# Scores and exponential emitted one opening sooner in each slot of a sparse graph transformer

## The chip, the cores and the metric

The kernel runs on one core of a Trainium2 chip, as one launch. The metric is the device time of that launch in microseconds (us); lower is better. The time before is the median of 7 runs. Five engines work in parallel, each through its own queue in order: TensorE (PE in the profile, with its weight loads as PEld), VectorE (DVE), ScalarE (ACT), GpSimd (POOL) and SyncE (SP, which issues direct DMAs; the gathers are issued by POOL).

## The reference

Sixteen graphs share one sparse adjacency matrix of 1024 nodes (an edge with probability 1/128); every node has 128 features. Four layers follow each other: layers 0, 2 and 3 are attention over the neighbours with 8 heads of 16, layer 1 is a graph attention with one additive score. Cut to what matters, an attention layer is

```python
Q, K, V = (h @ Wq), (h @ Wk), (h @ Wv)          # 8 heads of 16
scores = einsum('bnhd,bmhd->bhnm', Q, K) / sqrt(16)
attn = softmax(where(adj == 0, -inf, scores))
x = layer_norm(h + einsum('bhnm,bmhd->bnhd', attn, V) @ Wo + bo)
x = layer_norm(x + relu(x @ W1 + b1) @ W2 + b2)
```

and layer 1 takes `leaky_relu(h @ a_src + (h @ a_dst).T)` as scores, with `h = x @ W`, and a layer norm after the residual.

## The kernel before, in words

`sparse_path` does the work (`dense_path` is there for matrices with too many neighbours, and is not entered here). It sorts the nodes by their degree into 8 tiles of 128 (`t`), so that the nodes of a tile have about as many neighbours, and handles the 16 graphs in two groups of 8 (`g`). Keys and values of all nodes lie in tables in DRAM; the neighbours' rows are gathered by index.

**Units and parts.** A unit is (layer, group, tile): 64 in all. Four neighbours of 32 nodes fill the 128 partitions (a "chunk"), and `ROUNDS` says how many chunks a tile needs. A part of an attention unit is two chunks (L531 to L534): the tiles of a group have 10, 6, 6, 6, 4, 4, 4 and 3 parts. There are 3 attention layers, so six such groups of 8 units, and 258 attention parts. Layer 1 has parts of four chunks.

**A slot** is one pass of the loop at L735. For an attention part `i` it emits:

1. `products(i)`, L600: VectorE multiplies the gathered keys by the replicated queries.
2. `weighted(i - 1, 0)`, L639: VectorE multiplies the gathered values of the part before by its exponentials.
3. `gathered(i + 2)`, L591: two gathers on POOL, for a buffer that an earlier part has left.
4. `others()`: an opening, here called the first one.
5. in the second slot of a unit: the rest of `closing`. This is `divided` of the unit before: after its denominators (L680, L685) a reciprocal (L687) and two multiplications (L690) on VectorE, an addition on POOL (L700), and the start of two tails, one for each half of the group. Then the load of `x` two units ahead (L546) and the start of `queries(u + 1)`.
6. `others()`: the second opening.
7. `exponentials(i)`: VectorE sums the products over each head (L614, the scores), ScalarE takes the exponential (L618).
8. `summed(i - 1)`, L666: PE adds the weighted values up over the chunks of a round. In the first slot of a unit the denominators of the unit before follow.
9. `others()`: the third opening.

**Tails and fronts.** What follows the attention of a unit (output projection, two layer norms, feed-forward, projection for the next layer's table) is a generator, `attention_tail`, cut by `yield` into some 16 steps; two run at a time, the second a step behind. `others` advances both, as often as `pace` has grown by 1 (L763 to L765: 16 steps spread over three openings per part of the unit), and one step of `queries` for the next unit. The steps, in order: transposition (L429) and its eviction (L431); output projection (L465, L466); bias (`y`, L469, VectorE); squares (L413, ScalarE, four activations); the power -1/2 (L419, POOL); scaling (L422, ScalarE) with the next transposition and eviction (L433); first feed-forward matrix (L479) and its evictions (L483); second matrix (L488, L492); squares, power and scaling again; eviction, and the table rows of the next layer (L371 and L375, or L391 to L400), or in layer 3 two multiplications on POOL and a scattered store (L446 to L448). `queries` makes four matmuls (L566), a copy (L570), four replications over the neighbours (L575) and four copies (L578), for each half.

**Order.** The loop stands under `tc.manual_schedule()`: every engine executes its instructions in the order in which the program emits them. An instruction that waits holds back all behind it on its engine.

Of the kernel before, what the change touches and what calls it, by code (L numbers as in the profile page):

```python
# [76 lines left out]
def sparse_path(ctx: ExitStack, tc: tile.TileContext, a: dict, out: bass.AP, flag):  # L77
# [434 lines left out]
    def first(g):  # L512

        for t in range(T):
            for h in range(HF):
                xg = ones_.tile([P, GH, D], F32, tag="xg", name="xg")
                nc.gpsimd.indirect_dma_start(
                    out=xg.rearrange("p g d -> p (g d)"), out_offset=None,
                    in_=a["x"].rearrange("n (k c) -> (n k) c", k=GR * HF),
                    in_offset=bass.IndirectOffsetOnAxis(ap=places[:, g, h, t : t + 1], axis=0),  # L520
                )
                xn = states.tile([P, GH, P], F32, tag="xT", name="xT")
                turned(xg, xn)
                yield
                yield from project(0, g, t, h, xn)
# [11 lines left out]
    def is_attention(u):  # L537
        return LAYERS[units[u][0]][1] is ATTN

    def loaded(u):  # L540

        if u >= len(units):
            return
        l, g, t = units[u]
        xs[units[u]] = inputs.tile([P, HF, GH, P], F32, tag="x", name="x")
        nc.sync.dma_start(  # L546
            xs[units[u]].rearrange("p h g n -> p (h g n)"),
            kept[l, g][t].rearrange("p h c -> p (h c)"),
        )

    def queries(u):

        l, g, t = units[u]
        if not is_attention(u):
            ps = bank([P, J, G])
            for j in range(J):
                nc.tensor.matmul(ps[:, j, :], rep_of(j, True), srcs[g, t], start=True, stop=True)
            ofs[u] = smalls.tile([P, J, G], F32, tag="of", name="of")
            nc.scalar.copy(ofs[u], ps)
            return  # L560
        qs[u] = reps.tile([P, J, ROW], F32, tag="qr", name="qr")
        for h in range(HF):
            q = ones_.tile([P, GH * D], F32, tag="q", name="q")
            ps = bank([P, GH, D])
            for i in range(GH):
                nc.tensor.matmul(  # L566
                    ps[:, i, :], xs[l, g, t][:, h, i, :], w[LAYERS[l][0], "Wq"],
                    start=True, stop=True,
                )
            nc.scalar.copy(q, ps.rearrange("p g d -> p (g d)"))  # L570
            yield
            pss = []
            for j in range(J):
                ps = bank([P, GH * D])
                nc.tensor.matmul(ps, rep_of(j), q[32 * j : 32 * j + 32], start=True, stop=True)  # L575
                pss.append(ps)
            for j in range(J):
                nc.scalar.copy(qs[u][:, j, h * GH * D : (h + 1) * GH * D], pss[j])  # L578
            yield

    def gathered(i):
        if i >= len(parts):
            return
        u, r, j, n = parts[i]
        l, g, t = units[u]
        width = tables[l, g].shape[1]
        many = 2 if is_attention(u) else J
        e = gather_buffer()
        es[i] = e[:, : many * width].rearrange("p (k c) -> p k c", k=many)
        for k in range(n):  # L590
            nc.gpsimd.indirect_dma_start(  # L591
                out=es[i][:, k, :], out_offset=None, in_=tables[l, g][:, :],
                in_offset=bass.IndirectOffsetOnAxis(ap=idx[:, t, j + k, r : r + 1], axis=0),
                bounds_check=N - 1, oob_is_err=False,
            )

    def products(i):
        u, r, j, n = parts[i]
        prs[i] = [prods.tile([P, 2, ROW], F32, tag="pr", name="pr")]
        nc.vector.tensor_tensor(  # L600
            prs[i][0][:, :n, :], es[i][:, :n, :ROW], qs[u][:, j : j + n, :], ALU.mult
        )

    def exponentials(i):
        u, r, j, n = parts[i]
        t = units[u][2]
        heads = H if is_attention(u) else 1
        sc = smalls.tile([P, es[i].shape[1], G * heads], F32, tag="sc", name="sc")
        if u not in exs:
            exs[u] = exps.tile([P, max(map(sum, ROUNDS)), G * heads], F32, tag="ex", name="ex")  # L610
        c = CHUNK[t, r, j] - CHUNK[t, 0, 0]
        ex = exs[u][:, c : c + n, :]
        if is_attention(u):
            nc.vector.tensor_reduce(  # L614
                sc[:, :n, :], prs[i][0][:, :n, :].rearrange("p k (a d) -> p k a d", d=HD),
                mybir.AxisListType.X, ALU.add,
            )
            nc.scalar.activation(ex, sc[:, :n, :], AF.Exp, scale=1.0 / HD**0.5)  # L618
        else:
            nc.vector.tensor_tensor(  # L620
                sc[:, :n, :], es[i][:, :n, ROW:], ofs[u][:, j : j + n, :], ALU.add
            )
            nc.vector.scalar_tensor_tensor(
                sc[:, :n, :], sc[:, :n, :], SLOPE, sc[:, :n, :], ALU.mult, ALU.max
            )
            nc.scalar.activation(ex, sc[:, :n, :], AF.Exp)
# [79 lines left out]
    def advance(gens):  # L706
        for gen in list(gens):
            if next(gen, "end") == "end":
                gens.remove(gen)
# [3 lines left out]
    def others():  # L713
        pace[0] += pace[1]
        while pace[0] >= 1.0:
            advance(tails)
            pace[0] -= 1.0
        if fronts:
            advance(fronts)
        elif slow:  # L720
            advance(slow)

    with tc.manual_schedule():
        for _ in first(0):
            pass
        loaded(0)
        loaded(1)
        for _ in queries(0):
            pass
        slow.append(first(1))  # L730
        for i in range(AHEAD):
            gathered(i)
        closing = None
        begun = 0
        for i in range(len(parts) + 1):  # L735
            here = i < len(parts)
            u = parts[i][0] if here else len(units)
            if here:
                l = units[u][0]
                if i and parts[i - 1][0] != u:  # L740
                    begun = i
                    if units[u][1:] == (0, 1) and l + 1 < len(LAYERS):
                        if LAYERS[l + 1][1] is ATTN:
                            load_weights(LAYERS[l + 1][0])
                if is_attention(u):
                    products(i)
                else:
                    exponentials(i)
            ends = i + 1 >= len(parts) or parts[i + 1][0] != u
            if i:  # L750
                weighted(i - 1, 0)
                if not is_attention(parts[i - 1][0]):
                    others()
                    weighted(i - 1, 2)
                gathered(i - 1 + AHEAD)
            others()
            if closing is not None:
                while tails:
                    advance(tails)
                for _ in closing:  # L760
                    pass
                closing = None
                passes = 3 if is_attention(u) else 4  # L763
                steps = STEPS if is_attention(parts[begun - 1][0]) else GRAPH_STEPS
                pace[:] = 0.0, steps / (passes * sum(part[0] == u for part in parts) - 1)  # L765
            if here and u + 1 < len(units):
                if i == begun + 1:
                    loaded(u + 2)
                    fronts.append(queries(u + 1))
            others()  # L770
            if here and is_attention(u):
                exponentials(i)
            if i:
                summed(i - 1)
                if parts[i - 1][0] != u:
                    closing = divided(parts[i - 1][0])
                    next(closing)
            others()
            if ends:

                while fronts:
                    advance(fronts)
        while tails:
            advance(tails)
        for _ in closing:
            pass
        while tails:
            advance(tails)
# [434 lines left out]
```

## Time and profile before

| what | value |
|---|---|
| time, median of 7 runs (lowest to highest) | 3025.26 us (3013.36 to 3031.94) |
| profiled execution: its own time | 3021.78 us |
| profiled execution: span from the first to the last instruction | 3020.0 us |
| mean granted clock of TensorE | 0.845 |
| preparation before the first attention part | about 259 us |
| score sums L614: number, busy | 258, 561.7 us |
| exponentials L618: number, busy | 258, 81.1 us |
| products with keys L600 and with values L639, busy | 565.0 us and 760.2 us |
| gathers L591: number, busy on POOL, from issue to landing | 656, 886.3 us, 7.6 us |

The page of a profile gives the busy time of each engine, then the span in 40 slices, the DMA queues, the chain of work that ended last (followed back from the last instruction, at each step to what released it), and groups of instructions by line. The list of waits gives for each pair of lines how long one engine sat idle until the other's work was there. The timeline gives the instructions in order of time; in brackets stands the idle time in front of an instruction and who ended it. A window gives, for one stretch, the busy time of PE, PEld, DVE, ACT and POOL, then TensorE's granted clock, the share of the DMA engines and GB/s. Line numbers are those of the kernel.

### The profile page before, as it was taken

The page shows a single profiled execution, that of the slowest core. Times are in us where ns is not written, and L with a number is a line of the kernel's source. Part 1 is how long each engine was busy: PE and PEld are TensorE (multiplying, and loading weights), DVE is VectorE, ACT ScalarE, POOL GpSimd, SP SyncE. Part 2 cuts the span into 40 slices and gives each one's busy share as a digit, 9 for nine tenths or more (in the row PEclk, how much of TensorE's full clock was granted, in tenths as well). Part 3 has the DMA queues.
Part 4 walks back from the last instruction along what each step waited for, and adds up shares of the span by engine and source line. Part 5 has one row for each costly group of instructions (what it writes and reads, how often), then busy time and mean ns, then how long its engine had stood idle before and what let it go on. Part 6 is the DMA issues. An engine that isn't in the chain of part 4 may idle for free.

```text
span 3020.0 us, 35305 instructions
## 1 busy us (share of the span) xinstructions
PE 2123.1 (70%) x12569; PEld 1320.3 (44%) x12569; DVE 2150.4 (71%) x1493; ACT 1424.2 (47%) x4468; POOL 1478.2 (49%) x1086
## 2 busy tenths in 40 slices
PE   1365667776777776776577887787877666766766
PEld 1343445443554443434245554455544444333444
DVE  7505758668886666675788768887678877788772
ACT  1033345563556544445345664456543554434454
POOL 0123434433444568786335443454435577466673
PEclk9986888888788888978688988889887888777887
DMA  1057866546565568777665654766546554355540
GB/s 57 12 179 288 298 226 231 182 170 229 222 239 184 174 208 292 272 268 274 226 235 215 230 207 174 278 221 226 204 183 246 200 201 154 152 221 212 195 144 22
DMA packets 171144, 615.36 MB, mean 204 GB/s; under 512 B 44472, under 2 KB 47928, under 8 KB 122462
## 3 DMA queue, kind: packets, MB, share of 16 engines
q0 software_dynamic: 99584, 480.93, 43.9%
q1 hardware_dynamic: 71376, 132.10, 11.9%
q8 instruction: 101, 1.65, 0.2%
q14 instruction: 83, 0.68, 0.1%
HBM read 650.67 MB, written 100.73 MB: 249 GB/s over the span
## 4 chain that ended last, share of the span: by engine, by line
PE 38%; ACT 14%; DVE 13%; POOL 10%; issue 10%; DMA 7%; POOLq 0%; DVEq 0%; SPq 0%; ACTq 0%
PE ps L479 7%; PE yps L488 5%; ACT z L413 5%; PE ps L429 5%; PE acc L666 5%; DVE pr L639 4%; POOL e L591 4%; DVE sc L614 4%; POOL rstd L419 4%; DMA e<-table,idx 3%; DVE pr L600 3%; ACT qr L578 3%; PE yps L465 3%; PE ps L575 3%; PE yps L492 3%
## 5 line engine op out<-in xcount | busy, mean ns | idle before, releaser
L591 POOL DMA_INDIRECT e<-table,idx x656 | 886.3, 1351 | 442.2 <-DVE pr L639 258.5
L639 DVE TENSOR_TENSOR pr<-e,ex 128x2048 f32<-128x2048 f32 (+1 forms) x344 | 760.2, 2217 | 334.9 <-ACT ex L618 329.4
L419 POOL TENSOR_TENSOR rstd<-total,power 128x4 f32<-128x4 f32 x224 | 359.1, 1605 | 744.5 <-ACT z L413 711.4
L600 DVE TENSOR_TENSOR pr<-e,qr 128x2048 f32<-128x2048 f32 (+1 forms) x258 | 565.0, 2190 | 190.6 <-ACT qr L578 138.4
L666 PE MATMUL acc<-pr,marks 128*32 128x512 f32 x2624 | 468.5, 701 | 142.5 <-DVE pr L639 131.8
L614 DVE TENSOR_REDUCE sc<-pr 128x128 f32<-128x2048 f32 (+1 forms) x258 | 561.7, 2177 | 0.0
L429 PE MATMUL ps<-ident,z 128*128 128x128 f32 x768 | 198.0, 365 | 241.9 <-ACT z L422 241.9
L429 PEld LDWEIGHTS ps<-ident,z 128*128 128x128 f32 x768 | 126.3, 171 | 393.0 <-ACT z L422 320.3
L479 PE MATMUL ps<-x,W 128*128 128x512 f32 x384 | 245.6, 773 | 39.9 <-ACT x L433 39.9
L371 PE MATMUL ps<-Wkv,xT 128*128 128x256 f32 x768 | 239.1, 457 | 39.1 <-ACT xT L431 21.1
L488 PE MATMUL yps<-W,f 128*128 128x128 f32 x1536 | 255.3, 284 | 12.6 <-ACT f L483 10.6
L666 PEld LDWEIGHTS acc<-pr,marks 128*32 128x32 f32 x2624 | 89.3, 120 | 394.0 <-issue 213.9
L488 PEld LDWEIGHTS yps<-W,f 128*128 128x128 f32 x1536 | 209.2, 194 | 68.4 <-ACT f L483 43.2
L483 ACT ACTIVATE f<-ps,b 128x512 f32<-128x512 f32 x192 | 131.4, 687 | 224.6 <-PE ps L479 223.9
L578 ACT COPY qr<-ps 128x512 f32<-128x512 f32 x384 | 197.5, 596 | 76.4 <-PE ps L575 76.3
L413 ACT ACTIVATE z<-y,root 128x128 f32<-128x128 f32 x512 | 198.5, 396 | 51.2 <-DVE y L506 37.9
L575 PE MATMUL ps<-q,rep 32*128 32x512 f32 x768 | 172.2, 687 | 66.7 <-ACT oT L431 40.4
L371 PEld LDWEIGHTS ps<-Wkv,xT 128*128 128x128 f32 x768 | 161.9, 225 | 86.9 <-ACT xT L431 29.5
L618 ACT ACTIVATE ex<-sc 128x128 f32<-128x128 f32 (+1 forms) x258 | 81.1, 314 | 248.6 <-DVE sc L614 248.4
L465 PE MATMUL yps<-Wo,oT 128*128 128x128 f32 x768 | 182.0, 325 | 7.5 <-ACT oT L431 7.5
L422 ACT ACTIVATE z<-y,rstd 128x128 f32<-128x128 f32 x512 | 162.7, 391 | 31.0 <-POOL rstd L419 31.0
L375 ACT COPY kv<-ps 128x512 f32<-128x512 f32 x192 | 112.3, 586 | 136.8 <-PE ps L371 132.9
(128 smaller groups left out, 2951.7 us busy)
## 6 DMA issues: line engine op xcount, KB each, us to landing
table<-kv SPq DMA_DIRECT2D x96, 512.0 KB, 8.6
kept<-xT SPq DMA_DIRECT2D x128, 256.0 KB, 5.6
x<-kept SPq DMA_DIRECT2D x64, 512.0 KB, 9.9
e<-table,idx POOLq DMA_INDIRECT x656, 7.6
table<-kv SPq DMA_DIRECT2D x32, 256.0 KB, 6.2
edges<-in_adj SPq DMA_DIRECT2D x8, 512.0 KB, 3.9
W<-in_L_gnn_W SPq DMA_DIRECT2D x6, 128.0 KB, 2.7
xg<-in_x,places POOLq DMA_INDIRECT x32, 4.1
```

The costliest lines, as they stand in the source:

```text
L371: nc.tensor.matmul(ps[:, k, :], x[:, i + k, :], w[LAYERS[l][0], "Wkv"], start=True, stop=True,)
L413: nc.scalar.activation(z[:, i, :], y[:, i, :], AF.Square, scale=D**-0.5, bias=root, accum_out=total[:, i : i + 1],)
L419: nc.gpsimd.tensor_tensor(rstd, total, power, ALU.pow)
L429: nc.tensor.transpose(ps[:, i, :], z[:, i, :], ident)
L479: nc.tensor.matmul(ps, p["W1"][:, f * P : (f + 1) * P], x1.rearrange("p g n -> p (g n)"), start=True, stop=True,)
L488: nc.tensor.matmul(ps[:, i, :], f1[:, f, i * P : (i + 1) * P], p["W2"][:, f, :], start=(f == 0), stop=False,)
L578: nc.scalar.copy(qs[u][:, j, h * GH * D : (h + 1) * GH * D], pss[j])
L591: nc.gpsimd.indirect_dma_start(out=es[i][:, k, :], out_offset=None, in_=tables[l, g][:, :], in_offset=bass.IndirectOffsetOnAxis(ap=idx[:, ...
L600: nc.vector.tensor_tensor(prs[i][0][:, :n, :], es[i][:, :n, :ROW], qs[u][:, j : j + n, :], ALU.mult)
L614: nc.vector.tensor_reduce(sc[:, :n, :], prs[i][0][:, :n, :].rearrange("p k (a d) -> p k a d", d=HD), mybir.AxisListType.X, ALU.add,)
L639: nc.vector.tensor_tensor(prs[i][k0 // 2][:, :m, :].rearrange("p k (a d) -> p k a d", d=d), es[i][:, k0 : k0 + m, base : base + ROW].rearr ...
L666: nc.tensor.matmul(accums[u][32 * j : 32 * j + 32, h, :], marks[:, CHUNK[t, r, j], :], tiles[j // 2][:, j % 2, h * GH * D : (h + 1) * GH * D],
```

## The change

The call of `exponentials(i)` for attention parts moves from behind the second opening to in front of it, ahead of the block that finishes the unit before and ahead of the start of the next queries. Nothing else changes; the parts of layer 1 emit their exponentials at the head of the slot, as before.

```diff
                 gathered(i - 1 + AHEAD)
             others()
+            if here and is_attention(u):
+                exponentials(i)
             if closing is not None:
                 while tails:
                     advance(tails)
...
                     loaded(u + 2)
                     fronts.append(queries(u + 1))
             others()
-            if here and is_attention(u):
-                exponentials(i)
             if i:
                 summed(i - 1)
                 if parts[i - 1][0] != u:
```

## The prediction

> **What bounds the kernel now.** I read the page first, then the list of waits, then the timeline of single units of nodes engine by engine, and the chain of waits inside such a unit. No engine is full:
>
> ```profile
> PE 2123.1 (70%) x12569; PEld 1320.3 (44%) x12569; DVE 2150.4 (71%) x1493; ACT 1424.2 (47%) x4468; POOL 1478.2 (49%) x1086
> ...
> PE 38%; ACT 14%; DVE 13%; POOL 10%; issue 10%; DMA 7%; POOLq 0%; DVEq 0%; SPq 0%; ACTq 0%
> ```
>
> The fullest engine works 71% of the span, and the chain that ended last (second line) passes through all of them: the time is a chain of hand-overs, and what a shift is worth depends on who waits at the place. The list of waits (engine and line, whom it waited for: total us, times, longest) has both sides of the moved step:
>
> ```profile
> DVE pr L639 <- ACT ex L618: 329.4, 126, 8.9
> ...
> ACT ex L618 <- DVE sc L614: 248.4, 72, 18.0
> ```
>
> VectorE waits 329 us for the exponential, because ScalarE still has tail work in front of it; ScalarE waits 248 us for the score sums, with its tail work behind. The change trades the first against the second.
>
> The timeline of a unit of six parts, ScalarE and then VectorE (start us, duration us, line, idle before and who ended it):
>
> ```profile
> 820.08 1.28 ACT L422 ACTIVATE z<-y,rstd 128x128 f32<-128x128 f32 x4 [0.21 <-POOL rstd L419]
> 821.37 0.31 ACT L618 ACTIVATE ex<-sc 128x128 f32<-128x128 f32 x1
> ...
> 827.34 0.78 ACT L433 ACTIVATE x<-ps,ln_b,ln_g 128x512 f32<-128x512 f32 x1
> ...
> 831.79 0.69 ACT L483 ACTIVATE f<-ps,b 128x512 f32<-128x512 f32 x1 [0.17 <-PE ps L479]
> 832.37 0.30 ACT L618 ACTIVATE ex<-sc 128x128 f32<-128x128 f32 x1
> ...
> 837.90 1.15 ACT L422 ACTIVATE z<-yps,rstd 128x128 f32<-128x128 f32 x4
> 838.90 0.35 ACT L618 ACTIVATE ex<-sc 128x128 f32<-128x128 f32 x1
> ```
>
> ```profile
> 819.06 2.28 DVE L614 TENSOR_REDUCE sc<-pr 128x128 f32<-128x2048 f32 x1
> ...
> 825.67 2.27 DVE L614 TENSOR_REDUCE sc<-pr 128x128 f32<-128x2048 f32 x1
> ...
> 832.70 2.29 DVE L639 TENSOR_TENSOR pr<-e,ex 128x2048 f32<-128x2048 f32 x1 [2.56 <-ACT ex L618]
> ...
> 839.31 2.28 DVE L639 TENSOR_TENSOR pr<-e,ex 128x2048 f32<-128x2048 f32 x1
> ```
>
> The exponential at 832.37 had its sums at 827.94 and stood behind two L483 evictions of the second opening, so VectorE lost 2.56. But the next one (838.90) follows tail squares, and no reordering around the second opening brings it before these.
>
> **The change part by part.** Nothing is added or removed: 258 score sums (L614, mean 2.28) and 258 exponentials (L618, 0.31) move ahead of the second opening, and in the second slot of a unit ahead of the closing block too. They issue no DMA and nothing on PE, POOL or SP; those queues keep their order. On VectorE they pass L687, two L690 and at times one L469; on ScalarE the second opening's evictions, squares and scalings. Behind the exponential now wait these, and for them PE and POOL. Busy sums: 0. The attention units are 6 groups of 8, with 10, 6, 6, 6, 4, 4, 4 and 3 parts (43 x 6 = 258), so I price each kind once.
>
> *Six parts (18 units).* At the start L687 and both L690 now stand behind a sum of 2.2. The transposed output's eviction L431 (804.06) stood behind that slot's exponential (803.85) anyway, and the new sequence brings it at 803.9: nothing, hidden by the exponential; without that cover 2.2. In the third slot the L422 scaling at 820.08 must now wait for the sum's end (821.34) and 0.31: 1.57 late. The product before it loses its own wait (0.45 behind the L578 copies), so 1.1. PE restarts 1.1 us earlier without the pause after its first L575 matmuls; its clock:
>
> ```profile
> 804.00:806.00 2.00, 1.32 (x2) 0.50 (x2) 2.00 (x2) 2.00 (x5) 0.00 (x0) 0.50 1.04 419
> ...
> 810.00:812.00 2.00, 2.00 (x20) 2.00 (x19) 1.65 (x2) 0.85 (x2) 0.99 (x1) 0.99 0.58 226
> ```
>
> (After the five engines' busy times comes the granted clock: 0.50 for six us from the restart, then 0.99.) Its four L465/L466 pairs take 0.85 each at 0.50 and 0.45 at 0.99, 1.6 in all; whether an unbroken restart saves them no row shows: between 0 and 1.6, I take 0.8. That leaves 0.3 of lateness. In the fifth slot the exponential comes straight after the squares (end 838.02), 0.9 sooner than 838.90. The 2.56 saved before is lost again there. Per unit -0.9 + 0.3 = -0.6, taken as -0.5; ends -1.5 (clock kept) and +0.7 (none of it: 1.57 - 0.9). In layer 3 the first product also waits for a gather behind POOL's output work: 0 there (-0.9 to +0.7). Sum 12 x -0.5 = -6 (-23 to +12).
>
> *Four parts (18 units).* The chain inside one such unit, then POOL's timeline:
>
> ```profile
> 569.38 1.55 ACT z L413 x8
> ...
> 588.55 0.99 POOL e L591
> 589.57 3.05 POOL rstd L419
> ```
>
> ```profile
> 569.06 1.03 POOL L419 TENSOR_TENSOR rstd<-total,power 128x4 f32<-128x4 f32 x1 [7.33 <-ACT z L413]
> ```
>
> The second tail's squares (569.28) now wait for the sum's end (570.02) and the exponential: 1.06 late, less 0.21 for the exponential that no longer follows them, 0.85. In layers 2 and 3 the same places give 1.77, and 1.5 after that exponential. Later in the unit an exponential moves from 584.66 to 578.9, and VectorE's 5.25 wait goes, but its next product still waits for scalings at 592.64. What is freed is the place where L600 ran: it moves from 589.42 to about 585, and the POOL power beside it at 589.57, on the chain with 3.05, could cost the 1.03 that one costs without a product beside it: -2.0. The first power now meets that product and pushes the gathers: +0.35. Net relief 1.65. Layer 0: 0.85 - 1.65 = -0.8; layer 2: -0.15; layer 3, with output work behind the powers, 0. Sum -6; ends per unit +1.5 (no relief) and -2.2 (the gather's 2.08 beside a product back to 0.99 too): -40 to +23.
>
> *Ten parts (4 of 6 units have tails to hide).* Here VectorE is the chain (its lines are over half of it from 2203 to 2240). Its 1.51 wait at 2217.51 goes, and the sum of the second slot finishes in the wait before: 1.45 more. ScalarE then holds an eviction (2232.37) behind a later sum; I take -2.4 of the -3.0. Sum -10 (-12 to 0).
>
> *Three parts (6).* L433 at 2177.12 waits for the sum's end 2178.06 and 0.31: 1.25 late, after 0.6 at the start; the last exponential comes 1.7 sooner. I take +0.6 (0 to 1.85): +4 (0 to +11).
>
> Total -6 - 6 - 10 + 4 = -18. The profiled execution took 3021.78 (span 3020.00 and 1.78 around it): 3003.8. The median of the runs is 3.5 above it: 3007.
>
> [...]
>
> **The rivals.** *VectorE gains its waits:* if the squares of the fifth slot came earlier, the six-part units would keep the waits (2.56 to 3.65, mean 3.0, 18 units: 54) and the ten-part units 10: 2961. For it: 329 us of waiting at L639. Against: the squares at 836.5 wait for PE.
>
> *A mere rotation:* in a steady unit each engine repeats the same sequence; if all gains and losses meet at the next wait, 3025. For it: the 2.56 above is lost six us later. That the move does not reach the chip is not likely: in the trace the exponentials stand exactly where the program emits them.
>
> *ScalarE blocked (slower):* the tail work behind the exponential sets the end and neither relief comes, POOL's second power staying near 3.0 and PE at 0.50 as now. Then 6 x 0.85 + 12 x 1.5 (four parts) + 6 x 1.85 (three) + 12 x 0.7 (six) = 43, less 10: +33, 3058. It decides as soon as the powers that follow the late squares still meet a product. For it: 711 us in which L419 waits for squares. Against: after the move VectorE has its products done by then.
>
> **How the numbers follow.** Forecast 0.39, VectorE's waits 0.09, rotation 0.16, ScalarE blocked 0.36. Predicted 3007, its own range 2985 to 3016. With the ends of the unknown costs (-75 to +46, so 2950 to 3071) and no more than 2 in 10 left out, the range is 2962 to 3062. A difference below 0.3% (9 us) can't be told from none here. Faster 0.39 + 0.09 = 0.48, same 0.16, slower 0.36.
>
> **What would show it.** Right: the waits of L639 for L618 fall below 150 us, those of L618 for L614 rise above 248; the second L419 in four-part units takes about 1 us; granted clock above 0.50 at the first L465 of six-part units; ten-part units some 2 us shorter. Wrong: four-part periods (40.7 now, the reciprocals at 558.0 and 598.7) grow; L429's wait for L422 (242 us) grows, which is the blocked tail; or six-part periods (48.4, L687 at 799.68 and 848.11) change by more than 1.5.

## The result and the profile after

The changed kernel takes 3037.03 us (median of 18 runs) against 3022.98 (46 runs of the kernel before): ratio 1.0048, 95% interval 1.0039 to 1.0058. It is slower by some 14 us. The profiled executions differ by 8.2 us (span 3020.0 and 3028.2).

The page after, busy time by engine and then the chain that ended last:

```profile
PE 2105.1 (70%) x12569; PEld 1314.8 (43%) x12569; DVE 2146.3 (71%) x1493; ACT 1425.3 (47%) x4468; POOL 1537.7 (51%) x1086
...
PE 37%; DVE 20%; issue 11%; ACT 10%; DMA 7%; POOL 6%; POOLq 0%; DVEq 0%; SPq 0%; ACTq 0%
```

VectorE and ScalarE have the work that they had; only the order has changed, and VectorE's share of the chain rose from 13% to 20%. POOL is busy for 59.5 us more, though its instructions are the same: the gathers L591 took 955.3 us in all (886.3 before), the powers L419 336.4 (359.1). The list of waits after:

```profile
POOL rstd L419 <- ACT z L413: 794.7, 165, 18.4
...
ACT ex L618 <- DVE sc L614: 330.4, 112, 18.8
PE ps L429 <- ACT z L422: 268.2, 88, 8.7
DVE pr L639 <- ACT ex L618: 254.2, 84, 9.5
```

The exchange took place: VectorE waits 75 us less for the exponential (329.4 before), ScalarE 82 us more for the sums (248.4). TensorE waits 26 us more for the scalings (241.9), POOL 83 more for the squares (711.4): the tails are late.

Where the time went shows when the span is cut at the reciprocals L687, one for each unit. The stretch that ends at a unit's reciprocal, after less before, summed by kind (us; in layers 0, 2 and 3):

| kind of unit | units | forecast | measured |
|---|---|---|---|
| ten parts | 5 (the first unit apart) | -10 | +4.5 |
| six parts | 18 | -6 | -20.3 |
| four parts, layers 0 and 2 | 12 | -6 | +2.7 |
| four parts, layer 3 | 6 | 0 | +10.5 |
| three parts | 6 | +4 | +14.1 |

The six-part units gained more than forecast, the ten-part ones nothing; the short ones lost it all and more. (These kinds sum to 11.5 us, the whole spans differ by 8.2: the stretches of layer 1 and the ends make up the rest.)

**The third slot of a four-part unit** (layer 2), ScalarE and then TensorE. Before:

```profile
1674.80 0.56 ACT L570 COPY q<-ps 128x512 f32<-128x512 f32 x1
1675.27 0.40 ACT L413 ACTIVATE z<-y,root 128x128 f32<-128x128 f32 x1
...
1678.92 1.28 ACT L422 ACTIVATE z<-y,rstd 128x128 f32<-128x128 f32 x4
```

```profile
1676.49 1.92 PE L666 MATMUL acc<-pr,marks 128*32 128x512 f32 x16
1679.38 1.20 PE L429 MATMUL ps<-ident,z 128*128 128x128 f32 x4 [0.97 <-ACT z L422]
1681.45 1.99 PE L479 MATMUL ps<-x,W 128*128 128x512 f32 x4 [0.87 <-ACT x L433]
```

After:

```profile
1660.81 0.59 ACT L570 COPY q<-ps 128x512 f32<-128x512 f32 x1
1662.77 0.31 ACT L618 ACTIVATE ex<-sc 128x128 f32<-128x128 f32 x1 [1.38 <-DVE sc L614]
1662.99 0.39 ACT L413 ACTIVATE z<-y,root 128x128 f32<-128x128 f32 x1
...
1666.43 1.28 ACT L422 ACTIVATE z<-y,rstd 128x128 f32<-128x128 f32 x4
```

```profile
1662.51 1.92 PE L666 MATMUL acc<-pr,marks 128*32 128x512 f32 x16
1666.89 1.35 PE L429 MATMUL ps<-ident,z 128*128 128x128 f32 x4 [2.45 <-ACT z L422]
1669.11 3.78 PE L479 MATMUL ps<-x,W 128*128 128x512 f32 x4 [0.87 <-ACT x L433]
```

The squares L413 of the second tail used to follow the copy L570 at once; now they stand behind an exponential that waits 1.38 for its sum. TensorE, done with the sums L666, waits 2.45 instead of 0.97, and then its first four feed-forward matrices take 3.78 instead of 1.99. The windows of the same stretch (PE, PEld, DVE, ACT, POOL busy, then the granted clock, DMA share, GB/s) say why, before and then after:

```profile
1678.00:1680.00 2.00, 1.03 (x7) 0.31 (x3) 1.13 (x2) 2.00 (x7) 1.82 (x2) 1.00 0.14 53
1680.00:1682.00 2.00, 1.13 (x4) 0.55 (x5) 2.00 (x2) 1.58 (x5) 2.00 (x1) 1.00 0.00 0
1682.00:1684.00 2.00, 2.00 (x10) 1.14 (x8) 2.00 (x2) 1.77 (x4) 1.29 (x2) 1.00 0.52 94
```

```profile
1664.00:1666.00 2.00, 0.44 (x6) 0.00 (x0) 2.00 (x2) 2.00 (x8) 1.05 (x2) 1.00 0.25 101
1666.00:1668.00 2.00, 1.11 (x4) 0.60 (x4) 2.00 (x2) 1.71 (x6) 2.00 (x1) 0.89 0.00 0
1668.00:1670.00 2.00, 1.13 (x2) 0.50 (x2) 2.00 (x2) 1.72 (x5) 1.07 (x2) 0.50 0.63 127
```

Behind the pause the clock is 0.50; before, it was 1.00 throughout. Those four matrices take over 2.5 us in 17 of the 18 four-part units after, and in 7 before.

**The reciprocal in layer 3**, VectorE, before and after:

```profile
2547.51 3.33 DVE L639 TENSOR_TENSOR pr<-e,ex 128x2048 f32<-128x2048 f32 x1 [2.31 <-ACT ex L618]
2550.77 0.54 DVE L687 RECIPROCAL both<-both 128x64 f32<-128x64 f32 x1
```

```profile
2539.11 3.32 DVE L639 TENSOR_TENSOR pr<-e,ex 128x2048 f32<-128x2048 f32 x1 [5.94 <-ACT ex L618]
2542.36 2.27 DVE L614 TENSOR_REDUCE sc<-pr 128x128 f32<-128x2048 f32 x1
2544.55 0.54 DVE L687 RECIPROCAL both<-both 128x64 f32<-128x64 f32 x1
```

Here VectorE is last: in all six such units the reciprocal followed the last product at once, and now a whole sum, 2.2 us, lies between them. In layers 0 and 2 the reciprocal of a four-part unit had waited 0.27 to 1.04 us for its denominators, which hides a part of the sum.

**A three-part unit** (the last one of layer 3), the first eviction L433 after and before:

```profile
2964.78 0.31 ACT L618 ACTIVATE ex<-sc 128x128 f32<-128x128 f32 x1 [3.72 <-DVE sc L614]
2964.99 0.76 ACT L433 ACTIVATE x<-ps,ln_b,ln_g 128x512 f32<-128x512 f32 x1
```

```profile
2957.61 0.78 ACT L433 ACTIVATE x<-ps,ln_b,ln_g 128x512 f32<-128x512 f32 x1 [0.56 <-PE ps L429]
```

From the unit's reciprocal (2947.01 and 2943.17) it is 17.98 instead of 14.44: 3.5 us behind a sum that VectorE could not start sooner.

### The profile page after: what moved, and what is told of

The parts are those of the page before. It is cut to its first block, busy times and chain, and to the rows that moved or that the text cites. A ratio compares the mean times of both kernels' runs of the same rounds, so it can differ in the third digit from the quotient of the medians.

```text
span 3028.2 us, 35325 instructions
## 1 busy us (share of the span) xinstructions
PE 2105.1 (70%) x12569; PEld 1314.8 (43%) x12569; DVE 2146.3 (71%) x1493; ACT 1425.3 (47%) x4468; POOL 1537.7 (51%) x1086
## 3 DMA queue, kind: packets, MB, share of 16 engines
q8 instruction: 101, 1.65, 0.2%
## 4 chain that ended last, share of the span: by engine, by line
PE 37%; DVE 20%; issue 11%; ACT 10%; DMA 7%; POOL 6%; POOLq 0%; DVEq 0%; SPq 0%; ACTq 0%
PE ps L479 8%; DVE sc L614 8%; PE yps L488 6%; DVE pr L600 6%; PE ps L429 5%; DVE pr L639 5%; PE acc L666 4%; DMA e<-table,idx 4%; ACT z L413 4%; POOL e L591 4%; PE yps L492 3%; PE yps L465 2%; PE yps L466 2%; PE ps L371 2%; PE ps L575 2%
## 5 line engine op out<-in xcount | busy, mean ns | idle before, releaser
L591 POOL DMA_INDIRECT e<-table,idx x656 | 955.3, 1456 | 319.9 <-issue 169.7
L639 DVE TENSOR_TENSOR pr<-e,ex 128x2048 f32<-128x2048 f32 (+1 forms) x344 | 758.8, 2213 | 265.5 <-ACT ex L618 254.2
L419 POOL TENSOR_TENSOR rstd<-total,power 128x4 f32<-128x4 f32 x224 | 336.4, 1503 | 814.1 <-ACT z L413 794.7
L614 DVE TENSOR_REDUCE sc<-pr 128x128 f32<-128x2048 f32 (+1 forms) x258 | 561.7, 2177 | 0.0
L666 PE MATMUL acc<-pr,marks 128*32 128x512 f32 x2624 | 457.0, 698 | 128.0 <-DVE pr L639 118.5
L429 PE MATMUL ps<-ident,z 128*128 128x128 f32 x768 | 200.8, 372 | 268.2 <-ACT z L422 268.2
L429 PEld LDWEIGHTS ps<-ident,z 128*128 128x128 f32 x768 | 130.1, 176 | 421.3 <-ACT z L422 340.5
L479 PE MATMUL ps<-x,W 128*128 128x512 f32 x384 | 258.1, 809 | 64.9 <-ACT x L433 64.9
L371 PE MATMUL ps<-Wkv,xT 128*128 128x256 f32 x768 | 246.4, 468 | 41.4 <-ACT xT L431 23.3
L666 PEld LDWEIGHTS acc<-pr,marks 128*32 128x32 f32 x2624 | 87.4, 121 | 378.0 <-issue 211.2
L618 ACT ACTIVATE ex<-sc 128x128 f32<-128x128 f32 (+1 forms) x258 | 79.2, 307 | 331.0 <-DVE sc L614 330.4
L413 ACT ACTIVATE z<-y,root 128x128 f32<-128x128 f32 x512 | 198.7, 399 | 45.6 <-DVE y L506 36.2
L371 PEld LDWEIGHTS ps<-Wkv,xT 128*128 128x128 f32 x768 | 166.7, 232 | 91.5 <-ACT xT L431 31.8
L465 PE MATMUL yps<-Wo,oT 128*128 128x128 f32 x768 | 171.8, 309 | 8.0 <-ACT oT L431 7.9
L413 ACT ACTIVATE z<-yps,root 128x128 f32<-128x128 f32 x384 | 135.6, 368 | 85.1 <-PE yps L492 85.1
L575 PE MATMUL ps<-q,rep 32*128 32x512 f32 x768 | 156.1, 706 | 22.5 <-ACT q L570 21.9
```

What stands on the lines that cost most here:

```text
L371: nc.tensor.matmul(ps[:, k, :], x[:, i + k, :], w[LAYERS[l][0], "Wkv"], start=True, stop=True,)
L413: nc.scalar.activation(z[:, i, :], y[:, i, :], AF.Square, scale=D**-0.5, bias=root, accum_out=total[:, i : i + 1],)
L419: nc.gpsimd.tensor_tensor(rstd, total, power, ALU.pow)
L429: nc.tensor.transpose(ps[:, i, :], z[:, i, :], ident)
L465: nc.tensor.matmul(ps[:, i, :], oT[:, i, :], p["Wo"], start=True, stop=False)
L479: nc.tensor.matmul(ps, p["W1"][:, f * P : (f + 1) * P], x1.rearrange("p g n -> p (g n)"), start=True, stop=True,)
```

## The experiments

Each kernel is the changed one, with a condition for the early place; a part that doesn't meet it has its exponential behind the second opening, as before:

```diff
             others()
+            early = False
             if here and is_attention(u):
-                exponentials(i)
+                t, slot = units[u][2], i - begun
+                early = CONDITION
+                if early:
+                    exponentials(i)
...
             others()
+            if here and is_attention(u) and not early:
+                exponentials(i)
```

`slot` counts from 0. Theory A in the expectations is what the traces suggest: two places do the harm (the third slot, by lateness and the clock; the second, by the sum in front of the reciprocal), and the rest gains. The table has the ratio to the kernel before, on the same chip, and what the stretches of the profiled execution gained or lost against before (us). Units whose order is unchanged differ too: the 18 four-part ones in `long_units` by +5.7 in all (0.3 each), the six three-part ones in `by_kind` by +3.3 (0.6 each), the five ten-part ones in `mixed_b` by +10.3 (2.1 each). The stretches are all against one profile of the kernel before, whose median was 3022.98 to 3037.36 us in the different series; the ratio takes that out, the other columns don't.

| kernel | ratio, 95% interval | ten | six | four, layers 0, 2 | four, layer 3 | three |
|---|---|---|---|---|---|---|
| changed | 1.0048 (1.0039 to 1.0058) | +4.5 | -20.3 | +2.7 | +10.5 | +14.1 |
| not_third | 0.9924 (0.9902 to 0.9946) | +7.5 | -6.0 | -22.5 | +2.7 | +6.9 |
| only_third | 1.0141 (1.0123 to 1.0159) | -2.1 | -5.2 | +22.4 | +13.7 | +11.6 |
| second_mid | 1.0337 (1.0324 to 1.0350) | +3.3 | +12.2 | +39.2 | +18.0 | +34.1 |
| long_units | 0.9911 (0.9898 to 0.9923) | +5.3 | -23.5 | +3.4 | +2.3 | -2.1 |
| mixed_a | 0.9871 (0.9852 to 0.9889) | +5.2 | -25.3 | -27.6 | +4.1 | +0.8 |
| mixed_b | 0.9875 (0.9858 to 0.9892) | +10.3 | -19.9 | -24.3 | -7.6 | +0.4 |
| only_second | 1.0094 (1.0078 to 1.0110) | +4.0 | +4.3 | +12.5 | +12.3 | +7.7 |
| refilled | 1.0036 (1.0022 to 1.0049) | +2.0 | -7.8 | -5.6 | +6.6 | +16.2 |
| refilled_twice | 1.0105 (1.0076 to 1.0135) | +5.4 | -14.5 | +12.5 | +39.7 | +17.1 |
| by_kind | 0.9839 (0.9814 to 0.9863) | +3.5 | -18.4 | -26.5 | -5.4 | +3.3 |
| by_kind_refilled | 0.9875 (0.9854 to 0.9896) | +4.3 | -19.9 | -13.5 | -2.8 | -0.9 |
| filled_behind | 0.9947 (0.9927 to 0.9966) | +7.6 | -16.0 | -17.0 | +2.3 | +13.1 |
| third_early_filled | 0.9869 (0.9845 to 0.9894) | +8.1 | -18.7 | -21.5 | -2.5 | 0.0 |
| third_old_filled | 0.9813 (0.9786 to 0.9841) | +5.9 | -21.1 | -30.3 | -5.7 | +1.1 |

### The third slot

```diff
+                early = slot != 2    # not_third
+                early = slot == 2    # only_third
```

> The early place in every slot of an attention unit except the third, which keeps the old one; nothing is left out of the computation. Theory A (one slot does the harm: in the third slot the second tail's squares stand behind a late exponential, TensorE pauses longer and starts the feed-forward at half clock; the other slots gain): layer-0 four-part units, 40.7 us before and 41.1 changed, fall to 37 to 39.5, four matrices of the feed-forward at about 17.5 us after the reciprocal instead of 18.3; total 2985 to 3012, faster than before. Rival B (ScalarE is blocked a little in every slot, so the loss is spread over 258 slots): 48 of them go back, the loss shrinks from 14.5 to about 12, total near 3035, four-part units near 41.

> The early place in the third slot of each attention unit alone. Theory A: the harm without the gains: four-part units 1 to 3 us longer than before (42 to 44), three-part units 1 to 3 longer; total 3045 to 3075. Rival B: a fifth of the loss, total near 3026, units within 0.5 us of before.

Measured: 3006.11 and 3068.24 us. One slot of each unit turns a loss of 0.5% into a gain of 0.8%, and alone it costs 1.4%; rival B falls by both. In layer 0, not_third's four-part units take 38.8 us on the mean, as A expected. That the clock has a part in it isn't shown here: in not_third 10 of the 18 four-part units still ran slow first matrices (2.71 us on the mean, against 3.50 in the changed kernel and 2.56 before).

### The kinds of units

```diff
+                early = t < 4    # long_units
```

> The early place in the units of ten and six parts only, the old one in those of four and three. Theory A (the harm is in the short units alone, by their tails): the units of six parts keep their mean gain of 1.1 us, 18 of them 20 us, the short ones go back to their times before; total 2998 to 3010. Rival E (the loss is one of the whole chip, such as a lower clock of TensorE under this order): about half of it remains, total 3028 to 3034.

Measured: 3003.99 us. The six-part units keep their gain (-23.5), and the three-part ones, at the old place, lose nothing (-2.1 in place of +14.1). Rival E falls.

### The second slot

```diff
+                early = slot == 1    # only_second
```

> The early place in the second slot of each attention unit alone, where it is ahead of the reciprocal. Theory A: layer-3 four- and three-part units 1.3 to 2.2 us longer than before (the sum's 2.2 on the chain), those of layers 0 and 2 within 0.7; total 3033 to 3045. Rival G (as forecast: the transposed output's eviction stood behind the exponential anyway, so the place costs nothing): all units within 0.5, total 3022 to 3030.

Measured: 3051.35 us, beyond the expectation. In layer 3 the four-part units lose 12.3 us, 2.05 each: the sum in front of the reciprocal, as expected, but not it alone. All six ran slow first matrices there (3.3 us on the mean; 2.7 before, where three did), which is 0.6 each and leaves some 1.5 for the sum. A second comparison agrees: not_third and mixed_b (below) differ in these units in the second slot alone, and are 10.3 us apart, 1.7 each, of which the first matrices explain 0.4. Those of layers 0 and 2 lose 1.0 each where 0.7 was the bound. Rival G, which is the prediction's own reading, falls.

second_mid keeps the early place, but in the second slot emits `exponentials(i)` behind the closing block and ahead of the second opening:

> As the changed kernel, but in the second slot of each unit the sum and the exponential come behind the closing block (reciprocal, two multiplications) and still ahead of the second opening. Theory A also says that in layer 3 the sum of 2.2 us stands on the chain ahead of the reciprocal in the four-part units: with the sum behind it, these (43.4 to 44.2 changed) fall by 1 to 2.2, in layers 0 and 2 nothing moves by more than 0.5; total 3022 to 3032. Theory C (the sum ahead of the reciprocal costs in every short unit): all four- and three-part units fall by about 2, total near 2990. Theory D (its place there is of no account): 3037, all units as in the changed kernel within 0.5.

Measured: 3133.33 us. All three theories fell. The unit in layer 0 shows why (VectorE, ScalarE, then TensorE):

```profile
557.77 1.29 DVE L690 TENSOR_TENSOR o<-acc,both 128x512 f32<-128x512 f32 x2
558.98 2.27 DVE L614 TENSOR_REDUCE sc<-pr 128x128 f32<-128x2048 f32 x1
```

```profile
561.29 0.31 ACT L618 ACTIVATE ex<-sc 128x128 f32<-128x128 f32 x1 [2.49 <-issue]
561.50 0.57 ACT L431 COPY oT<-ps 128x512 f32<-128x512 f32 x1
```

```profile
558.61 0.63 PE L429 MATMUL ps<-ident,o 128*128 128x128 f32 x4 [0.35 <-DVE o L690]
...
562.12 0.49 PE L465 MATMUL yps<-Wo,oT 128*128 128x128 f32 x2 [1.99 <-ACT oT L431]
```

Behind the reciprocal the sum ends only at 561.2, and the exponential waits for it in front of the eviction L431 (the profile can't name the releaser and puts the 2.49 down to "issue"). The output projection begins 3.5 us after its transposition; in the changed kernel it is 1.4 (553.60 to 554.96). So in the second slot the early place has a price on either side of the closing block: the reciprocal waits for the sum, or the eviction for the exponential.

### The clock

refilled makes the replications just ahead of the pause twice, into the same banks; refilled_twice makes them three times:

```diff
+                for _ in range(2 if h and t in (5, 6, 7) else 1):    # refilled; 3: refilled_twice
+                    nc.tensor.matmul(ps, rep_of(j), q[32 * j : 32 * j + 32], start=True, stop=True)
-                nc.tensor.matmul(ps, rep_of(j), q[32 * j : 32 * j + 32], start=True, stop=True)
```

> The changed kernel with the four replications of the second half (L575) made twice in the units of four parts, each into the same bank: 1.15 us more of TensorE work in 18 units, just ahead of the pause before the second transposition (2.45 us in the changed kernel, 0.97 before). Nothing is left out of the computation. Theory A (the longer pause costs the clock, and the feed-forward's first matrices then take 3.6 us instead of 1.8): the clock stays at 1.00 there, four-part units fall by 1 to 1.8 in all three layers, total 3008 to 3025 although work is added. Rival H (the lateness of the second tail is all of it, the clock has no part): no unit falls, total 3037 to 3058.

Measured: 3032.98 us, inconclusive: the four feed-forward matrices took 2.0 us in 5 of the 18 units and 2.9 or more in the others. The pause was still 1.57; behind it the clock stayed at 1.00 in a unit of layer 0 and was 0.50 in units of layers 2 and 3.

> The changed kernel with the four replications of the second half made three times in the units of four parts: 2.3 us of TensorE work more in 18 units, which leaves a pause of 0.4 to 0.7 us where 1.57 were left with two, and the clock still fell in layers 2 and 3. Theory A (the pause costs the clock): 1.00 there in the four-part units of all three layers, first matrices of the feed-forward in 1.8 us; against that the copies L578 come up to 0.5 later; total 3005 to 3025. Rival H (the pause is not what lowers it): clock and units as with two, total 3033 to 3050.

Measured: 3059.82 us. It was no clean test: the four replications, 24 matmuls now, took 5.7 to 10.1 us where some 3.4 were reckoned with (three times the 1.15 of the expectation), and delayed everything behind them. The feed-forward's four matrices took 2.0 in 17 of the 18 units, but in three units of layer 0 and five of layer 3 the clock fell sooner, during the replications, while TensorE was busy (to 0.50 in the unit of the last section).

filled_behind puts the extra work where nothing waits for it, into the pause:

```diff
                 summed(i - 1)
+                if here and is_attention(u) and 4 <= units[u][2] <= 6 and i == begun + 2:
+                    ps = bank([P, P])
+                    for _ in range(7):
+                        nc.tensor.matmul(ps, ident, centre, start=True, stop=True)
```

> The changed kernel with seven matmuls of two constants (128x128, some 0.26 us each, 1.8 in all) into a bank of their own, behind the sums L666 of the third slot in each of the 18 units of four parts; nobody reads them. They lie in the pause itself, so nothing else is displaced. Theory A (the pause of 2.45 us ahead of the second transposition costs the clock): pauses below 1 us, clock 1.00 when the feed-forward starts, its four first matrices 2.0 us instead of 3.5 to 3.8, four-part units of every layer 1.5 to 2 shorter than in the changed kernel (0: from 41.1 to 39.2; 3: from 43.7 to 42); total 3005 to 3020. Rival H (the pause has no part in it, the clock falls by the load before): clock and units as in the changed kernel, total 3035 to 3050.

Measured: 3016.61 us. TensorE in the same place as above:

```profile
1671.62 1.92 PE L666 MATMUL acc<-pr,marks 128*32 128x512 f32 x16
1674.25 1.83 PE L778 MATMUL ps<-centre,ident 128*128 128x128 f32 x14 [0.71 <-ACT qr L578]
1676.00 1.21 PE L429 MATMUL ps<-ident,z 128*128 128x128 f32 x4
1678.08 1.98 PE L479 MATMUL ps<-x,W 128*128 128x512 f32 x4 [0.87 <-ACT x L433]
```

The matrices take 2.0 us in all 18 units (in the unit shown the granted clock is 1.00 from 1673 to 1681), and the four-part units fall from 42.0 to 40.4 us on the mean: 1.55 each, 28 us in all. 1.83 us of useless work in each of 18 units makes the changed kernel 1% faster, and faster than the kernel before. The clock's part is shown, rival H falls. Not all of it is new, though: 7 of the 18 units ran slow matrices in the kernel before. By the mean of these four matrices (2.56 us before, 3.50 changed, 1.98 filled) the change itself added 0.9 a unit, 17 us.

What the late squares cost by themselves is told by two kernels that differ in the third slot's place alone, with the pause filled in both (seven matmuls, or three where the pause is 0.97):

```diff
+                early = t < 4 or (t < 7 and (l < 3 or slot != 1))    # third_early_filled
+                early = t < 4 or (t < 7 and slot != 2 and (l < 3 or slot != 1))    # third_old_filled
```

> As filled_behind (seven matmuls of constants in the pause of the third slot of four-part units), with the early place kept for the units of ten and six parts and for those of four parts (in layer 3 not in the second slot); the old place in three-part units. If the later squares cost about 1 us a unit by themselves: four-part units 0.5 to 1.5 longer than in third_old_filled, total 2975 to 2990. If the clock was all of it: equal to third_old_filled or shorter by POOL's relief, 2955 to 2970.

> by_kind (third slot of four-part units at the old place) with three matmuls of constants behind the sums of that slot, into the pause of 0.97 us. The feed-forward's first four matrices took 2.0 to 3.7 us in by_kind's 18 units, 2.5 on the mean; with the pause filled 2.0 in all. If each unit keeps its account: 18 x 0.5 = 9 us below by_kind, ratio near 0.981, total 2960 to 2980. If the rest of the pauses lower the clock anyway: as by_kind, ratio near 0.984.

Measured: 2995.83 and 2981.57 us, intervals apart. The four-part units take 39.92 and 39.26 us: 0.66 each, and three of the latter's units still ran slow matrices (0.28 on the mean of 18). So the lateness costs 0.7 to 0.9 a unit, 12 to 17 us in all, about as much as the change's own part of the clock. Both totals lie just above what was expected (2975 to 2990, 2960 to 2980); the ratio of the second was met.

### Towards a better kernel

```diff
+                early = t < 4 or (t < 7 and l in (0, 2) and slot != 2)    # mixed_a
+                early = 0 < t < 4 or (3 < t < 7 and slot not in (1, 2))    # mixed_b
+                early = t < 4 or (t < 7 and slot != 2 and (l < 3 or slot != 1))    # by_kind
```

> Early place for the units of ten and six parts (all slots) and, in layers 0 and 2, for those of four parts in all slots but the third; the old place for the rest. Theory A (each unit keeps its own account): the gains of the two kernels add up, 23 us from the long units and 22 from the twelve four-part units; total 2978 to 2990, ratio near 0.985. Rival F (the chain hands a gain of one unit back in the next): no better than either of the two, near 3005.

> Early place for the units of six parts (all slots) and, in all three layers, for those of four parts in the first and last slot alone; the old place for the rest, the ten-part units too. Theory A (in layer 3 the sum stands ahead of the reciprocal in the second slot, and the last POOL power of the unit is relieved by the first and last slots): layer-3 four-part units fall 1 to 2.5 below before (not_third: 0.4 above), layer-0 ones stay at 38 to 39.5, ten-part units at their old times within 1; total 2970 to 2985. Rival (the second slot's early place brings the relief): four-part units lose the 2 us that they had gained, total 3000 to 3010.

> The places that each kind of unit did best with: early in all slots of the units of ten and six parts; in four-part units of layers 0 and 2 in all slots but the third, in those of layer 3 in the first and last slot; old elsewhere. If each unit keeps its own account: as mixed_a, less 11.7 us for the six layer-3 units (4.1 above before there, 7.6 below in mixed_b): total 2966 to 2976, ratio near 0.983. If the accounts are not separate: no better than 2981.

> by_kind with the replications of the second half made twice in the four-part units. Theory A: in the four-part units of layer 0 the clock stays at 1.00 at the feed-forward (0.50 in not_third), up to 1.8 us each; total 0 to 20 below by_kind, 2950 to 2976. Rival H: the added work costs, 0 to 15 above by_kind.

Measured: 2981.53, 2982.71, 2985.71 and 2990.45 us. The gains of the kinds add up nearly as expected; rival F falls. mixed_b's layer-3 units gain 1.3 each, and without the second slot's early place nothing is lost there. by_kind holds both (0.9839, expected near 0.983); its intervals overlap with those of mixed_a and mixed_b, so it isn't shown to be better than these. The replications made twice brought by_kind_refilled nothing: 0.9875, with an interval that touches by_kind's, and 11 of its 18 four-part units ran slow matrices (7 in by_kind), though the pause ahead of them was 0.74 instead of 0.97. third_old_filled is the fastest, 0.9813: 1.9% below the kernel before; against by_kind its interval overlaps.

## Why the prediction was wrong

The time of 3037 lies in the range (2962 to 3062), which is so wide that this says little; it isn't in the forecast's own (2985 to 3016), and the sign is the wrong one. Point by point:

- **"Busy sums: 0":** right for VectorE and ScalarE, whose busy times moved by -4.1 and +1.1 us; not for POOL (+59.5). A gather of the six-part units took 1.62 us instead of 1.37 on the mean, one of the ten-part units 1.35 instead of 1.13. What that costs was not tried.
- **Six parts, -6:** right in sign, too small (-20.3). The term was TensorE's restart, "between 0 and 1.6, I take 0.8": the first two products L465 of the first tail, with the L466 between them, take 0.94 us, at a granted clock of 1.00, instead of 1.65 in 8 of 18 units (2 before). The six units that changed from one to the other gained 13.3 of the 20.3; the layer-3 units, put at 0, gained 4.5 without it.
- **Four parts, -6: the step that failed.** The terms that it had were near: the squares come 1.24, 1.23 and 1.36 us late in layers 0, 2 and 3 (forecast 0.85, 1.77 and 1.5), and POOL's last power falls from 3.04 to 1.05 (forecast -2.0), here in layer 2, before and then after:

```profile
1695.55 3.05 POOL L419 TENSOR_TENSOR rstd<-total,power 128x4 f32<-128x4 f32 x1
```

```profile
1684.94 1.05 POOL L419 TENSOR_TENSOR rstd<-total,power 128x4 f32<-128x4 f32 x1
```

  Two terms were missing, the clock and the reciprocal of the next point. The lateness was carried to the next wait as if TensorE could idle for nothing; the pause grew from 0.97 to 2.45 and the clock behind it fell from 1.00 to 0.50. Filling the pause is worth 1.55 a unit, 28 us, of which some 17 are the change's own. The six-part paragraph had priced the clock behind a pause; this one had not.
- **"Nothing, hidden by the exponential":** the reciprocal's delay was priced once, in the six-part unit, and that answer was carried to all kinds. In layer 3's four-part units VectorE ends the chain, and the 2.2 named there as the price without cover is near what they lose (2.05 in only_second, some 1.5 without the clock's share). "Layer 3, with output work behind the powers, 0" became +10.5.
- **Ten parts, -10:** wrong (+4.5). VectorE's wait of 1.51 went, as forecast, but the next product waits for its gathers. The long wait at the end of one such stretch (layer 3), before and then after:

```profile
2261.11 2.29 DVE L600 TENSOR_TENSOR pr<-e,qr 128x2048 f32<-128x2048 f32 x1 [5.16 <-DMA e<-table,idx]
```

```profile
2251.63 2.29 DVE L600 TENSOR_TENSOR pr<-e,qr 128x2048 f32<-128x2048 f32 x1 [7.31 <-DMA e<-table,idx]
```

  In this stretch VectorE came to the wait 3.1 us sooner and lost 2.15 of them in it; the sum in front of the reciprocal took the rest and a little more. The longest such wait grew in all four stretches that have one (4.45 to 5.16 before, 7.11 to 7.36 after). No kernel took this wait away, and the ten-part units rose even more in mixed_b (+10.3), which leaves them at the old place; what lengthens them stays open.
- **Three parts, +4:** right in sign, too small (+14.1). "1.25 late" was read from one unit; L433 comes 0.7 to 1.4 late in four units and 3.4 to 3.5 in the two that have no queries to replicate, before layer 1 and at the end, where the squares are done sooner and the wait for the sum is longer. In layer 2, where L433 is 0.7 late, the units grew by 2.5; the clock at L371 was lower too (0.86 on the mean, 1.00 before), but its share was not tried.
- **What would show it:** right for L618 behind L614 (330.4) and for the power L419 that had taken 3.04, now 1.04 to 1.05 us in all 18 four-part units; half right for the clock at the first L465 of six-part units (above 0.50 in 8 of 18); wrong for L639 behind L618 (254, forecast below 150) and for the ten-part units. Both signs of error that concern the blocked tail came: longer four-part units, and L429's wait at 268.2.
- **The rivals:** the slower one had the sign and the late squares, but not the reason. It asked that POOL's relief fail to come; that came in full, and in layers 0 and 2 the lateness and the clock, which it had not, used it up.

The outcome hangs on more than the pause. Behind the same pauses of 0.97 and 0.87, 7 of the 18 four-part units before ran slow matrices (3.21 to 3.62 us) and eleven did not (1.98 or 1.99). In the changed kernel all 17 units with a pause of 1.68 or of 2.45 to 2.46 ran slow (2.95 to 3.78), and the one with 0.01 did not (1.98); in the unit of layer 2 above, 1.35 us of transpositions between pauses of 2.45 and 0.87 did not keep the clock at 1.00.

One measure, chosen after the fact, separates them in three of the kernels. In the trace before, all 266 records of the granted clock (1.00 or 0.50) begin on one grid of 3.41 us, to within 0.002 us. Take the stretch of that grid in which the four matrices start (if it ends within 1.6 us of their start) and the stretch before it, and of these the one in which TensorE is less busy: its busy share is 0.46 to 0.63 in the seven slow units before and 0.66 or more in the eleven others, 0.28 to 0.51 in the 17 slow ones after, and 0.74 or more in all 18 of filled_behind. It gives no bound: in refilled three units were fast at 0.54 to 0.55 and four slow at 0.54 to 0.63, and three units of third_old_filled were slow at 0.71 to 0.72. What sets the clock isn't shown.

## What to carry to other kernels

Price a moved instruction in each kind of unit by what stands behind it on both engines that it touches; an answer found in one kind ("hidden") doesn't hold in the next, where another engine ends the chain. Lateness that ended in a longer pause of TensorE had a second price here, the clock behind the pause (0.50 behind 2.45 us), and where the pause wasn't closed, 1.83 us of matmuls that nobody reads paid for themselves (1.55 off each four-part unit). An order that helps in some slots and hurts in others is best split: the same edit gave +0.5% everywhere and -1.6% with the place chosen by kind and slot.

## What was not expected of the hardware

In refilled_twice the clock fell with no pause over 0.73 us: the windows of a four-part unit in layer 0, and TensorE's timeline there.

```profile
572.00:574.00 2.00, 2.00 (x10) 1.23 (x10) 2.00 (x2) 1.43 (x8) 0.00 (x0) 0.80 0.27 105
574.00:576.00 2.00, 2.00 (x10) 1.34 (x7) 2.00 (x2) 1.00 (x4) 1.27 (x2) 0.50 0.00 0
```

```profile
571.24 9.28 PE L576 MATMUL ps<-q,rep 32*128 32x512 f32 x24 [0.73 <-ACT q L570]
```

TensorE counts as busy throughout, with 24 matmuls over 32 rows that took 9.28 us, while 16 of them take 2.02 in refilled (in a unit of layer 2, at a granted clock of 1.00, 24 took 5.74). Why the third copy costs so much, and whether the slow matmuls lower the clock or the other way round, was not tried.
